# One edge per query in blocks without TensorE, with q, k and v as one paced stream and output projections spread, in a sparse graph attention layer

## The chip, the cores and the metric

The kernel runs on one core of one Trainium2 chip. The metric is the device time of one execution in microseconds (us), lower is better. PE is TensorE, DVE is VectorE, ACT is ScalarE, POOL is GpSimd; SP is the engine whose queue issues the plain DMAs.

## The reference

One graph attention layer on 16 batches of 1024 nodes with 512 features, 8 heads of 64, all float32. Each query attends only to the nodes that the 0/1 matrix `adj` (1024 x 1024, the same for all batches) names in its row:

```python
q = (x @ Wq + bq).reshape(b, n, H, HD)
k = (x @ Wk + bk).reshape(b, n, H, HD)
v = (x @ Wv + bv).reshape(b, n, H, HD)
scores = jnp.einsum('bqhd,bkhd->bhqk', q, k) / jnp.sqrt(jnp.float32(HD))
scores = scores + (1.0 - adj)[None, None, :, :] * -1000000000.0
attn = jax.nn.softmax(scores, axis=-1)
out = jnp.einsum('bhqk,bkhd->bqhd', attn, v).reshape(b, n, d)
return out @ Wo + bo
# and around it
x = _layernorm(x + _L0_gnn_ref(x, adj, ...), axis=-1)
```

The inputs' `adj` has 4043 ones in 1024 x 1024. They are unevenly spread: the first 128 queries have 1404, the last 128 have 273, the largest row has 66, and 60 rows have none (there the softmax is uniform over all nodes, and the attention output is the mean of v).

## The kernel before, in words

It does not form the score matrix. The ones of `adj` are a list of edges (query, key). The 1024 queries are cut into 8 tiles of 128; the edges of tile t, in the order of their queries, are cut into `BLOCKS[t]` blocks of 128 edges, one edge to a partition. The table is (11, 6, 4, 4, 3, 3, 3, 3), 37 blocks a batch and 592 in all. A query without edges has one made-up edge, to a row N of the key table that holds zeros and the mean of v.

`edges(t)` runs once, in the first microseconds and into batch 0: from the rows of `adj` it makes `key_row` and `query_row` (for each edge the row to fetch) and `sums` (for each block a 128 x 128 matrix of zeros and ones that adds up the edges of one query).

For each batch, `front(b, t)` computes q, k and v of one tile of 128 nodes: four matmuls of 128 x 512 each for q, k and v (`product`, L377), a bias, and a write to tables in DRAM (`q_rows`, `kv_rows`, two of each, taken in turn by `b % 2`). DVE adds the biases of q and k (`out_q`, `out_k`), ACT copies v and squares q and k for a guard.

For each block n, these steps follow one another, each in its own turn of a loop:
- `gather(n)`: POOL issues two indirect DMAs, the q row of each edge (`qg`, L501) and its k and v row (`kvg`, L506), eight turns ahead.
- `scores(n)`: DVE multiplies q by k (L515) and adds up by head (L517). `exponentials(n)`: ACT takes exp (L522).
- `weigh(n)`: DVE multiplies v by the exponentials (L533); in batch 0 for every second block, and in batch 15 for two of three, ACT does it (L529).
- `add_up(n)`: PE multiplies the block's matrix from `sums` with the weighted v and the exponentials, in two matmuls (L545, L546), into the PSUM tile `sum` of the query tile.

After the last block of a query tile, `normalise` on DVE divides by the sum of the exponentials (L553, L554, L557). PE transposes the result (`poT`, L566), and `finish(b, t)` multiplies it by Wo (`po`, again L377). DVE adds x (L468) and takes mean and variance; POOL takes the root (L477), ACT scales (L482), SP writes the tile out. The tile of x for this is loaded again by `load_y` (tile `y`), and POOL adds the output bias to it (L461).

The order on every engine is written out by the loop at the end (`tc.manual_schedule()`), with one turn for each block; `later(k, fn)` puts work into a turn further on. In each turn the loop emits the block steps, then takes units of PE work from two lists while a credit lasts: `fronts` (a unit is one matmul of 128 x 512, or a transpose of x) and `finishing`. The credit of a turn (`share`) is set anew for each batch so that the lists run empty with the batch. `finishing` is only filled when `fronts` is empty, so each batch runs the fronts of the next batch first, and then the output projections one after the other. A first stretch of 34 turns without blocks (`LEAD_IN`) makes the edges, the fronts of batch 0 and part of batch 1.

PSUM has eight banks: two `sum` tiles of two banks each and four `fill` tiles of one bank, which all other matmuls share.

## Time and profile before

| | |
|---|---|
| median of 3 runs | 2595.01 us (2594.36 to 2597.61) |
| the profiled execution's own time, and its span | 2595.89 us, 2594.1 us |
| mean granted TensorE clock over the span | 0.982 |
| busy: PE, DVE, POOL, ACT | 2477.6, 1968.2, 1499.0, 698.7 us |
| 16 DMA engines: share of POOL's queue, of SP's queue | 56.3%, 21.2% |
| chain that ended last: PE, POOL, DVE, issue | 68%, 11%, 10%, 7% |

The span runs from the first to the last instruction. In the profile a float32 matmul is two PE instructions, so 512 matmuls of one kind stand as x1024. The spans of two matmuls in a row overlap, since they are pipelined: what a matmul costs PE when it is packed is the distance from its start to the next one's start. The blocks of batch 0 begin at 162.4 us, those of batch 1 at 309.5, and a batch takes about 153.5 us from then on; the last batch begins at 2458.5 us.

### The profile page before, as it was taken

The numbers are of one execution on the slowest core, as the hardware profiler recorded it, in microseconds if no ns is written. First come the engines' busy times: TensorE is split into PE (matmuls) and PEld (weight loads), VectorE is DVE, ScalarE is ACT, GpSimd is POOL, SyncE is SP. The second block draws the span as 40 slices with busy tenths as digits, with TensorE's granted clock in tenths as the row PEclk, the third lists the DMA queues.
The fourth block names the chain that finished last, engine by engine and source line by source line (L and its number), as shares of the span: only waits on it lengthen the run. The fifth ranks groups of instructions, "written<-read, shape, count | busy, mean of one in ns | idle before, by whom it ended". The sixth has DMA issues, their size and how long they took to land.

```text
span 2594.1 us, 26742 instructions
## 1 busy us (share of the span) xinstructions
PE 2477.6 (96%) x7659; PEld 1352.6 (52%) x7659; DVE 1968.2 (76%) x3613; ACT 698.7 (27%) x1764; POOL 1499.0 (58%) x1717
## 2 busy tenths in 40 slices
PE   6988999999999999999999999999999999999967
PEld 3545555555555555555555555555555555555534
DVE  5668778778778877877777777877877777787766
ACT  1345322222222222222222222222222222222254
POOL 0156755647566574756647465564756557475675
PEclk9989999999999999999999999999999999999978
DMA  4368887887879788787878878787887978878785
GB/s 154 110 243 290 270 291 247 286 270 271 283 237 307 254 291 267 257 292 244 301 253 292 271 235 306 244 294 256 277 288 233 309 251 287 264 256 287 230 277 179
DMA packets 228679, 678.01 MB, mean 261 GB/s; under 512 B 29454, under 2 KB 29466, under 8 KB 228524
## 3 DMA queue, kind: packets, MB, share of 16 engines
q0 software_dynamic: 132608, 465.64, 56.3%
q1 hardware_dynamic: 93344, 205.60, 21.2%
q10 hardware_dynamic: 2572, 4.99, 0.5%
q8 instruction: 62, 1.02, 0.2%
q14 instruction: 93, 0.76, 0.1%
HBM read 541.86 MB, written 134.25 MB: 261 GB/s over the span
## 4 chain that ended last, share of the span: by engine, by line
PE 68%; POOL 11%; DVE 10%; issue 7%; ACT 2%; DMA 1%; ACTq 0%; POOLq 0%; another core or an unknown queue 0%; SPq 0%; DVEq 0%
PE pv L377 16%; PE pk L377 15%; PE pq L377 15%; PE sum L546 7%; PE sum L545 7%; POOL kvg L506 4%; PE po L377 4%; POOL y L461 3%; POOL qg L501 2%; DVE y L468 2%; DVE stats L471 2%; PE pxT L359 2%; PE poT L566 2%; DVE qg L515 1%; DVE pv L533 1%
## 5 line engine op out<-in xcount | busy, mean ns | idle before, releaser
L501 POOL DMA_INDIRECT qg<-q_rows,query_row x592 | 586.9, 991 | 588.1 <-DVE s L517 453.7
L506 POOL DMA_INDIRECT kvg<-kv_rows,key_row x592 | 588.7, 994 | 195.2 <-issue 182.9
L533 DVE TENSOR_TENSOR pv<-kvg,pv 128x512 f32<-128x512 f32 x550 | 394.3, 717 | 223.1 <-ACT pv L522 146.8
L377 PE MATMUL pq<-wq,xT 128*128 128x512 f32 x1024 | 482.7, 597 | 14.7 <-ACT xT L363 13.2
L377 PE MATMUL pk<-wk,xT 128*128 128x512 f32 x1024 | 488.9, 598 | 7.1 <-ACT xT L363 7.1
L377 PE MATMUL pv<-wv,xT 128*128 128x512 f32 x1024 | 479.1, 593 | 0.0
L377 PE MATMUL po<-wo,oT 128*128 128x512 f32 x1024 | 473.9, 602 | 0.0
L515 DVE TENSOR_TENSOR qg<-qg,kvg 128x512 f32<-128x512 f32 x592 | 432.6, 731 | 0.3 <-issue 0.3
L517 DVE TENSOR_REDUCE s<-qg 128x8 f32<-128x512 f32 x592 | 406.1, 686 | 20.5
L545 PE MATMUL sum<-pv,sums 128*128 128x256 f32 x1184 | 361.6, 387 | 46.4 <-DVE pv L533 33.8
L545 PEld LDWEIGHTS sum<-pv,sums 128*128 128x128 f32 x1184 | 222.2, 192 | 326.5 <-issue 239.0
L522 ACT ACTIVATE pv<-s 128x8 f32<-128x8 f32 x592 | 124.1, 210 | 929.2 <-DVE s L517 626.5
L546 PE MATMUL sum<-pv,sums 128*128 128x264 f32 x1184 | 366.6, 392 | 4.6 <-ACT pv L529 2.3
L377 PEld LDWEIGHTS pk<-wk,xT 128*128 128x128 f32 x1024 | 194.3, 192 | 193.3 <-issue 175.7
L377 PEld LDWEIGHTS po<-wo,oT 128*128 128x128 f32 x1024 | 192.9, 194 | 182.6 <-issue 173.3
L377 PEld LDWEIGHTS pv<-wv,xT 128*128 128x128 f32 x1024 | 190.5, 191 | 167.0 <-issue 158.4
L377 PEld LDWEIGHTS pq<-wq,xT 128*128 128x128 f32 x1024 | 187.1, 192 | 159.2 <-issue 135.0
L546 PEld LDWEIGHTS sum<-pv,sums 128*128 128x128 f32 x1184 | 226.2, 192 | 41.6 <-ACT pv L529 6.4
L461 POOL TENSOR_TENSOR y<-y,bo_bc 128x512 f32<-128x512 f32 x128 | 163.4, 1277 | 141.5 <-ACT pv L522 74.7
L468 DVE TENSOR_TENSOR y<-po,y 128x512 f32<-128x512 f32 x128 | 88.0, 688 | 151.5 <-POOL y L461 139.4
L404 DVE TENSOR_TENSOR kv<-pk,bk_bc 128x512 f32<-128x512 f32 x128 | 88.2, 689 | 115.8 <-PE pk L377 87.2
L389 DVE TENSOR_REDUCE nrm<-sq 128x8 f32<-128x512 f32 x256 | 172.9, 676 | 1.4 <-ACT sq L388 1.4
(98 smaller groups left out, 1664.8 us busy)
## 6 DMA issues: line engine op xcount, KB each, us to landing
kv_rows<-kv SPq DMA_DIRECT2D x128, 512.0 KB
x<-in_x_dram SPq DMA_DIRECT2D x128, 256.0 KB
q_rows<-q SPq DMA_DIRECT2D x128, 256.0 KB
y<-in_x_dram SPq DMA_DIRECT2D x128, 256.0 KB
out_dram<-y SPq DMA_DIRECT2D x128, 256.0 KB
qg<-q_rows,query_row POOLq DMA_INDIRECT x592
kvg<-kv_rows,key_row POOLq DMA_INDIRECT x592
a<-in_adj_dram SPq DMA_DIRECT2D x8, 512.0 KB
```

What stands on the lines that cost most here:

```text
L377: nc.tensor.matmul(p, lhs()[:, ts(c, P)], w[:, c, :], start=(c == 0), stop=(c == NPAIR - 1))
L389: later(1, lambda: nc.vector.tensor_reduce(NRM[b][:, i, t, :], sq.rearrange("p (h d) -> p h d", d=HD), axis=AX.X, op=OP.add))
L461: later(2, lambda: nc.gpsimd.tensor_tensor(Y[b, t], Y[b, t], bo_bc, op=OP.add))
L468: nc.vector.tensor_tensor(y, p, y, op=OP.add)
L501: nc.gpsimd.indirect_dma_start(out=QG[n], out_offset=None, in_=q_rows[b % 2], in_offset=bass.IndirectOffsetOnAxis(ap=query_row[:, g:g + 1] ...
L506: nc.gpsimd.indirect_dma_start(out=KG[n], out_offset=None, in_=kv_rows[b % 2], in_offset=bass.IndirectOffsetOnAxis(ap=key_row[:, g:g + 1], ...
L515: nc.vector.tensor_tensor(m, m, KG[n][:, 0:D], op=OP.mult)
L517: nc.vector.tensor_reduce(S[n], m.rearrange("p (h d) -> p h d", d=HD), axis=AX.X, op=OP.add)
L522: nc.scalar.activation(PV[n][:, D:], S.pop(n), AF.Exp)
L533: nc.vector.tensor_tensor(pv[:, 0:D].rearrange("p (h d) -> p h d", d=HD), v[:, D:].rearrange("p (h d) -> p h d", d=HD), pv[:, D:, None].to ...
L545: nc.tensor.matmul(SUM[b, t][:, 0, 0:HD2], m, pv[:, 0:HD2], **kw)
L546: nc.tensor.matmul(SUM[b, t][:, 1, 0:HD2 + HEADS], m, pv[:, HD2:], **kw)
```

## The change

**The first edge of each query.** `edges` now gives the first edge of every query (with the made-up edges) a block of its own for each tile, in which edge and query stand on the same partition. Only the others go to the blocks with a `sums` matrix, and the table falls to (10, 5, 3, 3, 2, 2, 2, 2): 29 blocks with PE and 8 without, again 37 a batch. The block without PE is the last of its tile. Its q rows are a plain tile of `q_rows`, so SP loads them with a plain DMA; its k and v rows are gathered by POOL as before. It is scored and weighed as all blocks are (its `PV` has a pool of its own, `pv0`). `normalise`, now in the turn of that block, adds it to the PSUM sums on DVE and then divides.

**Places without an edge.** Where a block is not full, `key_row` is now 65536 instead of 0, and the gather of k and v has a limit of row N, beyond which nothing is fetched. The eight buffers of `kvg` are set to zero by POOL at the start.

**The order.** The fronts of all 16 batches are one list. The share of a turn now also pays for the sums (the constant `SUM` for each block with PE), and it is set so that the fronts run one batch and 14 turns (`EARLY`) ahead of the blocks' batch. Output projections no longer wait for an empty list: a tile's units come first once it is done and its `y` is loaded, at the least two turns after the tile before began; `y` is loaded for one tile at a time. The DRAM tables are three each (`ROWS`). PSUM has one `sum` tile and six `fill` tiles. `y` has 6 buffers (was 7), `oT` 5 (was 7).

```diff
-BLOCKS = (11, 6, 4, 4, 3, 3, 3, 3)
+BLOCKS = (10, 5, 3, 3, 2, 2, 2, 2)
+NO_ROW = 65536.0
+ROWS = 3
+EARLY = 14
+SUM = 0.87
...
-    NB = sum(BLOCKS)
+    NS = sum(BLOCKS)
+    NB = NS + NT
...
-            return psum.tile([P, HALF], F32, tag="fill", name=name, bufs=4)
+            return psum.tile([P, HALF], F32, tag="fill", name=name, bufs=6)
...
+            nc.vector.tensor_scalar(off, kl[:, 0:1], -1.0, 0.0, op0=OP.add, op1=OP.max)
+            nc.vector.tensor_scalar(key_row[:, NS + t:NS + t + 1], off, float(N), None, op0=OP.min)
...
+                nc.vector.tensor_scalar(e[:, 0, :], e[:, 1, :], 0.0, NO_ROW, op0=OP.is_lt, op1=OP.mult)
+                nc.vector.tensor_tensor(key_row[:, g0:g0 + n], e[:, 1, :], e[:, 0, :], op=OP.max)
...
+            if i == BLOCKS[t]:
+                g = NS + t
+                nc.sync.dma_start(QG[n], q_rows[b % ROWS][ds(t * P, P), :])
+            else:
+                g = first[t] + i
+                nc.gpsimd.indirect_dma_start(
+                    out=QG[n], out_offset=None, in_=q_rows[b % ROWS],
+                    in_offset=bass.IndirectOffsetOnAxis(ap=query_row[:, g:g + 1], axis=0),
+                )
...
                 in_offset=bass.IndirectOffsetOnAxis(ap=key_row[:, g:g + 1], axis=0),
+                bounds_check=N, oob_is_err=False,
...
-                SUM[b, t] = psum.tile([P, 2, HALF], F32, tag="sum", name=f"sum_{b}_{t}", bufs=2)
+                PSUM[b, t] = psum.tile([P, 2, HALF], F32, tag="sum", name=f"sum_{b}_{t}", bufs=1)
...
-            nc.vector.tensor_scalar(r, s[:, 1, HD2:HD2 + HEADS], 1.0e-30, None, op0=OP.max)
+            nc.vector.tensor_tensor(r, s[:, 1, HD2:HD2 + HEADS], pv[:, D:], op=OP.add)
+            nc.vector.tensor_tensor(
+                o.rearrange("p (a d) -> p a d", a=2), s[:, :, 0:HD2], pv[:, 0:D].rearrange("p (a d) -> p a d", a=2),
+                op=OP.add,
+            )
             nc.vector.reciprocal(r, r)
-            for i in range(2):
-                nc.vector.tensor_tensor(
-                    o[:, ts(i, HD2)].rearrange("p (h d) -> p h d", d=HD),
...
+            o8 = o.rearrange("p (h d) -> p h d", d=HD)
+            nc.vector.tensor_tensor(o8, o8, r[:, :, None].to_broadcast([P, HEADS, HD]), op=OP.mult)
...
+        for i in range(8):
+            nc.gpsimd.memset(work.tile([P, 2 * D], F32, tag="kvg", name=f"kvg_first_{i}", bufs=8), 0.0)
...
+                    left = sum(u[0] for u in fronts)
+                    goal = fronts_time - (n // NB + 2 + EARLY / NB) * batch_time
+                    share = (max(0.0, left - goal) + NT * NPAIR * PRODUCT + NS * SUM) / NB
...
+                if 0 <= n < total and blocks[n][2] == BLOCKS[blocks[n][1]]:
+                    normalise(n)
...
-                    if not fronts and not finishing and done and n > loaded.get(done[0], n):
+                    if not finishing and done and n > loaded.get(done[0], n) and n > last_finish + 1:
```

How it moves the engines' orders is seen at three places in the middle of batch 8. In the rows, the numbers in a name are batch and tile (`sum_8_6`: batch 8, tile 6) or the block (`pv_327`), and the last number tells buffers apart.

PE, tile 6 of batch 8, before. This stands late in the batch, where the fronts are used up:

```order
L545 MATMUL sum_8_6_10063<-pv_327_9978,sums_108 128x256
L546 MATMUL sum_8_6_10063<-pv_327_9978,sums_108 128x264
L377 MATMUL po_8_1_10025<-wo_69,oT_8_1_9708 128x512 x2
L377 MATMUL po_8_2_10070<-wo_69,oT_8_2_9813 128x512
L545 MATMUL sum_8_6_10063<-pv_328_10017,sums_108 128x256
L546 MATMUL sum_8_6_10063<-pv_328_10017,sums_108 128x264
L566 MATMUL poT_8_5_10099<-ident_58,o_8_5_10051 128x128 x4
L377 MATMUL po_8_2_10070<-wo_69,oT_8_2_9813 128x512 x3
L377 MATMUL po_8_3_10107<-wo_69,oT_8_3_9918 128x512
L545 MATMUL sum_8_6_10063<-pv_329_10061,sums_108 128x256
L546 MATMUL sum_8_6_10063<-pv_329_10061,sums_108 128x264
```

and the same tile now:

```order
L571 MATMUL sum_8_6_10750<-pv_327_10687,sums_108 128x256
L572 MATMUL sum_8_6_10750<-pv_327_10687,sums_108 128x264
L391 MATMUL po_8_4_10753<-wo_69,oT_8_4_10685 128x512
L591 MATMUL poT_8_5_10755<-ident_58,o_8_5_10705 128x128 x4
L391 MATMUL po_8_4_10753<-wo_69,oT_8_4_10685 128x512 x2
L571 MATMUL sum_8_6_10750<-pv_328_10721,sums_108 128x256
L572 MATMUL sum_8_6_10750<-pv_328_10721,sums_108 128x264
L391 MATMUL po_8_4_10753<-wo_69,oT_8_4_10685 128x512
L391 MATMUL pv_10_1_10728<-wv_67,xT_10_1_10497 128x512 x2
L373 MATMUL pxT_10_3_10785<-ident_58,x_10_3_10379 128x128 x4
L391 MATMUL pq_10_2_10826<-wq_63,xT_10_2_10656 128x512 x4
```

The third pair of sums of the tile is gone; units of a later batch's fronts (`pq_10_2`) and one tile's projection (`po_8_4`) stand between the sums, where three tiles' projections stood.

DVE, at the end of tile 5 of batch 8, before:

```order
L533 TENSOR_TENSOR pv_328_10017<-kvg_328_9830,pv_328_10017 128x512
L515 TENSOR_TENSOR qg_329_9854<-qg_329_9854,kvg_329_9856 128x512
L517 TENSOR_REDUCE s_329_10042<-qg_329_9854 128x8
L553 TENSOR_SCALAR rden_8_5_10048<-sum_8_5_9957 128x8
L554 RECIPROCAL rden_8_5_10048<-rden_8_5_10048 128x8
L557 TENSOR_TENSOR o_8_5_10051<-sum_8_5_9957,rden_8_5_10048 128x256 x2
L468 TENSOR_TENSOR y_8_0_9960<-po_8_0_9992,y_8_0_9960 128x512
```

and now:

```order
L559 TENSOR_TENSOR pv_327_10687<-kvg_327_10485,pv_327_10687 128x512
L537 TENSOR_TENSOR qg_328_10510<-qg_328_10510,kvg_328_10512 128x512
L539 TENSOR_REDUCE s_328_10703<-qg_328_10510 128x8
L579 TENSOR_TENSOR rden_8_5_10706<-sum_8_5_10662,pv_326_10660 128x8
L580 TENSOR_TENSOR o_8_5_10705<-sum_8_5_10662,pv_326_10660 128x512
L584 RECIPROCAL rden_8_5_10706<-rden_8_5_10706 128x8
L586 TENSOR_TENSOR o_8_5_10705<-o_8_5_10705,rden_8_5_10706 128x512
L484 TENSOR_TENSOR y_8_3_10629<-po_8_3_10665,y_8_3_10629 128x512
```

Two instructions of 128 x 512 stand where two of 128 x 256 stood, one turn earlier than before, and the final addition of tile 3 (`y_8_3`) follows directly, where it was tile 0's.

POOL now, from the second block of tile 5 of batch 8 on (`kvg_326` is the block without PE; before, a gather of `qg` stands ahead of every gather of `kvg`):

```order
L522 DMA qg_325_10417<-q_rows_2_118,query_row_110 128x512
L527 DMA kvg_325_10419<-kv_rows_2_115,key_row_109 128x1024
L477 TENSOR_TENSOR y_8_1_10385<-y_8_1_10385,bo_bc_72 128x512
L527 DMA kvg_326_10454<-kv_rows_2_115,key_row_109 128x1024
L493 TENSOR_TENSOR rstd_10435<-rstd_10435,neg_half_88 128x1
L494 TENSOR_TENSOR rstd_10435<-rstd_10435,mv_10432 128x1
L495 TENSOR_TENSOR rstd_10435<-rstd_10435,neg_one_90 128x1
L522 DMA qg_327_10483<-q_rows_2_118,query_row_110 128x512
```

The gather of `qg_326` is no longer on POOL; SP issues that load instead.

More of the change, by code (lines that the diff above doesn't have):

```diff
@@ L519, in exponentials @@
         def exponentials(n):
[L521 removed]
+            b, t, i = blocks[n]
+            if i == BLOCKS[t]:
+                PV[n] = work.tile([P, D + HEADS], F32, tag="pv0", name=f"pv_{n}", bufs=2)
+            else:
+                PV[n] = work.tile([P, D + HEADS], F32, tag="pv", name=f"pv_{n}", bufs=4)
             nc.scalar.activation(PV[n][:, D:], S.pop(n), AF.Exp)
@@ L585 @@
         with tc.manual_schedule():
-            gathered = 0
-            fronts, finishing = [], []
-            front_batches = 0
+            fronts = transpose_x(0, 0) + transpose_x(0, 1)
+            for b in range(B):
+                for t in range(NT):
+                    fronts += front(b, t)
+            fronts_time = sum(u[0] for u in fronts)
+            batch_time = fronts_time / B
+            finishing, last_finish = [], -LEAD_IN
             credit = 0.0
@@ L595 @@
                 now[0] = n
-                if front_batches < B and front_batches <= max(n // NB, 0) + 1:
-                    fronts += [u for t in range(NT) for u in front(front_batches, t)]
-                    front_batches += 1
                 if n < 0:
@@ L602 @@
                 elif n % NB == 0:
-                    tiles = len(done) + (NT if n + NB < total else NT + 2)
-                    share = (sum(u[0] for u in fronts) + tiles * NPAIR * PRODUCT) / NB
-                while gathered < min(n + AHEAD + 1, total) and blocks[gathered][0] in set_up:
-                    gather(gathered)
-                    gathered += 1
+                    left = sum(u[0] for u in fronts)
+                    goal = fronts_time - (n // NB + 2 + EARLY / NB) * batch_time
+                    share = (max(0.0, left - goal) + NT * NPAIR * PRODUCT + NS * SUM) / NB
+                while gathered[0] < min(n + AHEAD + 1, total) and blocks[gathered[0]][0] in set_up:
+                    gather(gathered[0])
+                    gathered[0] += 1
                 if 0 <= n + 1 < total:
```

82 lines of the change are left out of this document (37 added, 45 removed).

## The prediction

> **What bounds the kernel now.** I read the page's engine lines first, then PE's timeline, then one window for each stage.
>
> ```profile
> PE 2477.6 (96%) x7659; PEld 1352.6 (52%) x7659; DVE 1968.2 (76%) x3613; ACT 698.7 (27%) x1764; POOL 1499.0 (58%) x1717
> PE 68%; POOL 11%; DVE 10%; issue 7%; ACT 2%; DMA 1%; ACTq 0%; POOLq 0%; another core or an unknown queue 0%; SPq 0%; DVEq 0%
> L545 PE MATMUL sum<-pv,sums 128*128 128x256 f32 x1184 | 361.6, 387 | 46.4 <-DVE pv L533 33.8
> L546 PE MATMUL sum<-pv,sums 128*128 128x264 f32 x1184 | 366.6, 392 | 4.6 <-ACT pv L529 2.3
> ```
>
> PE is busy and carries the chain that ended last. But its spans overlap, so their lengths are not prices. The timeline of PE in the middle of a batch (start, length, operation) gives the prices:
>
> ```profile
> 1001.64 0.59 PE L545 MATMUL sum<-pv,sums 128*128 128x256 f32 x2
> 1002.07 0.61 PE L546 MATMUL sum<-pv,sums 128*128 128x264 f32 x2
> 1002.52 3.60 PE L377 MATMUL pv<-wv,xT 128*128 128x512 f32 x8
> 1005.95 0.59 PE L545 MATMUL sum<-pv,sums 128*128 128x256 f32 x2
> 1006.38 0.61 PE L546 MATMUL sum<-pv,sums 128*128 128x264 f32 x2
> 1006.83 0.60 PE L359 MATMUL pxT<-ident,x 128*128 128x128 f32 x4
> 1007.27 2.74 PE L377 MATMUL pq<-wq,xT 128*128 128x512 f32 x6
> ```
>
> From start to start: a block's sums take 1002.52 - 1001.64 = 0.88 us, four matmuls of 512 columns 1005.95 - 1002.52 = 3.43 (0.858 each), four transposes 0.44. Nothing lies between. A batch has 96 matmuls for q, k, v, 32 of `po`, 16 groups of transposes, one mean and 37 sums: 82.4 + 27.5 + 7.0 + 0.9 + 32.6 = 150.3 us of packed PE work. The windows by stage (length, then busy time of PE, PE's loads, DVE, ACT, POOL; clock; DMA share) tell where that is the limit:
>
> ```profile
> 0.00:162.40 162.40, 136.76 (x401) 67.10 (x402) 92.67 (x172) 47.69 (x84) 32.57 (x36) 0.98 0.44 155
> 162.40:309.50 147.10, 127.28 (x423) 73.60 (x422) 118.42 (x247) 73.40 (x232) 96.67 (x97) 0.92 0.79 269
> 309.50:460.00 150.50, 150.50 (x471) 82.90 (x470) 117.47 (x215) 34.80 (x83) 85.81 (x97) 1.00 0.81 268
> 920.30:1073.80 153.50, 151.31 (x470) 82.82 (x470) 121.15 (x217) 36.47 (x86) 92.31 (x106) 1.00 0.82 272
> 2458.50:2476.80 18.30, 10.32 (x25) 5.35 (x25) 9.79 (x19) 10.46 (x38) 14.40 (x21) 0.72 0.80 254
> 2476.80:2573.90 97.10, 72.06 (x211) 39.62 (x210) 67.72 (x126) 54.21 (x209) 66.74 (x77) 0.82 0.74 248
> 2573.90:2594.10 20.20, 11.23 (x33) 5.30 (x31) 8.00 (x27) 3.72 (x5) 7.41 (x15) 0.84 0.31 103
> ```
>
> Batch 1 takes 150.5 us and batch 5 (920.3 to 1073.8) 153.5, against 150.3 of packed work: from batch 1 to 14 the kernel is PE's stream and little else. In batch 0 the order before holds only 118.6 us of PE work at these prices, in 147.1; in batch 15 and the end about 61, in 135.6. There others set the pace.
>
> **The change part by part.**
>
> *Sums removed.* 8 blocks a batch lose their two matmuls: 8 x 0.88 = 7.0 us, and 128 x 0.88 = 112.6 in all. A full batch falls to 143.1 us. By the group rows above the same would be 4 x (0.387 + 0.392) = 3.1 us summed for a block, or 728.2 / 592 = 1.23 as busy time, 157 in all. The Trainium skill ("Perfetto Trace Analysis", its note ahead of "Sequencer Loop") calls matmul busy time a bad metric, because matmuls are pipelined; by busy time the kernel would end 45 us earlier than I say, and the timeline's 0.88 agrees with the page. I take 0.88.
>
> *Addition on DVE.* The timeline of DVE gives its prices:
>
> ```profile
> 1009.40 0.68 DVE L421 TENSOR_TENSOR vsum<-vsum,kv 128x512 f32<-128x512 f32 x1
> 1010.00 0.16 DVE L553 TENSOR_SCALAR rden<-sum 128x8 f32<-128x8 f32 x1
> 1010.20 0.20 DVE L554 RECIPROCAL rden<-rden 128x8 f32<-128x8 f32 x1
> 1010.43 0.75 DVE L557 TENSOR_TENSOR o<-sum,rden 128x256 f32<-128x256 f32 x2
> 1011.11 0.68 DVE L533 TENSOR_TENSOR pv<-kvg,pv 128x512 f32<-128x512 f32 x1
> 1011.71 0.68 DVE L515 TENSOR_TENSOR qg<-qg,kvg 128x512 f32<-128x512 f32 x1
> 1012.42 0.69 DVE L517 TENSOR_REDUCE s<-qg 128x8 f32<-128x512 f32 x1
> 1013.02 0.68 DVE L397 SCALAR_TENSOR_TENSOR q<-pq,bq_bc 128x512 f32<-128x512 f32 x1
> ```
>
> `normalise` takes 1011.11 - 1010.00 = 1.11 us. Now it has two small instructions (0.20 + 0.23) and two of 128 x 512, each between 0.60 (L533) and 0.71 (L515, whose successor needs its result): 1.63 to 1.85, and I take 1.75, nearer to the dependent one. So DVE gets 0.64 x 8 = 5.1 us a batch: 121.2 + 5.1 = 126 in a batch of about 145.6. That is hidden behind PE, with the cover thinner: 87% instead of 79%. Without cover it would cost 16 x 5.1 = 82 us. It is thinnest in the four tiles of three blocks: three blocks at 1.91 us, `normalise`, the layer norm of one tile (1.74 us) and about half a front tile (five instructions at 0.60 a tile, so 1.6) make 10.8 us of DVE beside 11.5 of PE.
>
> *Order.* The boundary of each batch has one stall (timeline, idle time and its releaser in brackets):
>
> ```profile
> 929.33 0.70 PE L545 MATMUL sum<-pv,sums 128*128 128x256 f32 x2 [1.90 <-DVE pv L533]
> 926.85 0.69 DVE L468 TENSOR_TENSOR y<-po,y 128x512 f32<-128x512 f32 x1 [5.37 <-POOL y L461]
> 928.60 0.68 DVE L533 TENSOR_TENSOR pv<-kvg,pv 128x512 f32<-128x512 f32 x1
> 911.08 1.28 POOL L461 TENSOR_TENSOR y<-y,bo_bc 128x512 f32<-128x512 f32 x1
> 916.43 1.27 POOL L461 TENSOR_TENSOR y<-y,bo_bc 128x512 f32<-128x512 f32 x1
> 925.55 1.27 POOL L461 TENSOR_TENSOR y<-y,bo_bc 128x512 f32<-128x512 f32 x1
> DVE y L468 <- POOL y L461: 139.4, 64, 5.4
> POOL y L461 <- DMA y<-in_x_dram: 40.4, 12, 8.2
> ```
>
> In the run of projections one after the other, POOL falls behind (5.3 us from one `y` to the next); DVE then waits 5.37 us for it, and 1.90 reach PE, so DVE runs some 3.5 us ahead. Spread projections give POOL three turns or more for each, and this stall should go. In its place small ones may come, since DVE is fuller and each `y` is loaded only two turns before POOL needs it. I take 2.5 us a batch, between the 0.2 of batch 1 and the 3.2 of batch 5.
>
> *POOL, SP, DMA.* POOL's timeline prices a gather:
>
> ```profile
> 999.98 0.94 POOL L501 DMA_INDIRECT qg<-q_rows,query_row  x1 [1.95 <-DVE s L517]
> 1001.22 0.94 POOL L506 DMA_INDIRECT kvg<-kv_rows,key_row  x1 [0.30 <-issue]
> 152.67 1.95 POOL L506 DMA_INDIRECT kvg<-kv_rows,key_row  x1 [0.30 <-issue]
> 11.39 2.34 POOL L276 TENSOR_TENSOR codes<-a,place 128x1024 f32<-128x1024 f32 x1 [8.07 <-DMA a<-in_adj_dram]
> ```
>
> A gather takes 1.24 us of POOL, start to start; eight fewer a batch free 10 us, so POOL, at 92 of 153.5, gets looser. SP issues the 128 q loads, each in the place where POOL's gather stood, eight turns ahead. Behind them on SP stand writes of q, k, v that themselves wait for DVE's later work of the same turn, so I cost the wait for a free `qg` buffer at nothing; at worst it makes the writes late, which have a whole batch to land. The limit on the gathers is not in the trace. Its bounds are minus the time of the roughly 633 rows a batch that are no longer fetched (3712 places with PE, 3079 edges), and, from above, the longest gather of batch 0 (1.95 us, 1.0 more than the usual one). I take zero: most gathers stand at 0.94, and PE hides either end. The eight memsets of `kvg` stand on POOL ahead of `codes`, in its wait of 8.07 us for `adj`; each writes as many elements as `codes`, which takes 2.34 us, so they cost between nothing and 8 x 2.34 - 8.07 = 10.7 us. I take nothing, since a memset reads nothing, and keep the rest for the range.
>
> *One `sum` tile.* The next tile's first sum waits until `normalise` has read PSUM: one turn (3.9 us) and the lead of 3.5 us against 2.7 of DVE. Nothing, as long as DVE leads.
>
> *Three tables, fronts further ahead.* This moves PE work from the end to batch 0. Counted in the changed order at the prices above, PE has 149.0 us in batch 0 (was 118.6), 136.7 in batch 1, 143.1 on average in 2 to 13, 110.5 in batch 14 and 58 in batch 15. Batch 0's idle PE was 28.5 us, partly three waits for rows of `adj`, such as
>
> ```profile
> 178.30 0.90 PE L338 MATMUL pof<-ident,of 128*128 128x128 f32 x3 [5.89 <-ACT kv L410]
> 222.80 2.08 PE L377 MATMUL pk<-wk,xT 128*128 128x512 f32 x2 [7.15 <-ACT xT L363]
> ```
>
> Those stay, a microsecond shorter each as the turns are longer; the one at the batch's end (about 5.7) goes: 28.5 - 3 - 5.7 = 19.8. The last 51 turns have no fronts, 37 before. There DVE (3.1 us a turn with ACT not helping in batch 14) and POOL set the pace: 3.3 us in the last 14 turns of batch 14, and 97.1 / 33 = 2.94 in batch 15.
>
> The sum of the stages: until batch 0 161 (was 162.4); batch 0 149.0 + 19.8 = 169; batch 1 136.7 + 2.5 = 139; batches 2 to 13 1717 + 12 x 2.5 = 1747; batch 14 86.4 + 1.5 + 14 x 3.3 = 134; batch 15 37 x 2.94 = 109, and the end 20. Together 2479 of span, against 2594.1. The profiled execution took 2595.89 us, 1.8 over its span, and the median of the runs 2595.01, 0.9 over it: 2480 us, 4.4% faster.
>
> **The rivals.**
>
> 1. *DVE becomes the bound in the short tiles.* If each `y` costs DVE its mean wait of 139.4 / 64 = 2.2 us, a three-block tile takes 13.0 us against 11.5, four of them lose 6 us a batch, 3.5 more than I allow, or with the `sum` tile chained behind it up to 6: 13 x 3.5 to 6 gives 2526 to 2558. For it speaks the 94% there; against it that batches 1 to 14 hide all such waits but one.
> 2. *The stalls go altogether.* Batches at 0.2 instead of 2.5, and half of batch 0's waits covered by six `fill` tiles: 2480 - 30 - 10 = 2440.
> 3. *Slower: the `y` chain.* Each tile now goes from load to POOL to DVE at the shortest distance. If each waits as the one at 926.85 does, a batch is 126 + 8 x 5.37 = 169 us of DVE, and the kernel about 2790. It decides against the change from a mean wait of (153.5 - 126) / 8 = 3.4 us; the mean was 2.2.
> 4. *The gather with a limit is dear on POOL.* POOL's work is 66 x 1.24 + 8 x (5.3 - 2.5) = 104 us a batch with its issue gaps; 1.1 us more on each of 37 gathers makes 146, where it starts to bind, and 1.35 eats the whole gain: 2480 to 2600.
> 5. *The end runs at half clock.* The clock is 0.72 to 0.84 in batch 15 and 1.00 in batch 5, and the stretch without fronts grows by 14 turns. At half clock throughout, PE's 24 + 58 us there double to 164, beside 46 + 129 = 175 us that the others need. If they overlap as now, that adds nothing; if half of the added 82 is exposed, the time is 2521. Against it: batch 15 kept its 2.94 us a turn at these clocks. The Trainium skill ("TensorE: Matmul & The Clock Gate", "HAM oscillation") says that gaps of more than about 3.4 us on PE halve its clock; by that rule the added turns run cold too, and the windows agree as far as they go.
>
> **How the numbers follow.** My sum 0.60, rival 1 0.13, rival 2 0.13, rival 3 0.05, rival 4 0.06, rival 5 0.03. For 8 in 10 the range takes in rivals 2 and 5 and most of rival 1: 2440 to 2545. About 0.2% can be told from no change here; slower comes from rival 3 and a third of 4 (0.07), the same from half of 4 (0.03), faster 0.90.
>
> **What would show it.** Right: sums x928 instead of x1184, batches of 144 to 147 us, PE packed in them, the idle stretch in the last 51 turns at 3.0 to 3.3 us each, DVE near 87%. Wrong: PE waiting for `pv` or `o` of DVE in the short tiles (rival 1), DVE waiting for `y` of POOL eight times a batch (3), a longer `kvg` gather (4). The prediction falls if a batch in the middle takes over 150 us.

## The result, and the profile after

| | before | after |
|---|---|---|
| median of 4 runs each | 2596.31 us (2594.36 to 2601.66) | 2467.62 us (2464.03 to 2469.3) |
| span of the profiled execution | 2594.1 us | 2466.9 us |

The ratio is 0.9499 (95% interval 0.9481 to 0.9518): 5.0% faster, where 2480 us and 4.4% were said. The page of the changed kernel (busy time, then the chain by engine, then two groups):

```profile
PE 2354.3 (95%) x7123; PEld 1259.7 (51%) x7123; DVE 2025.7 (82%) x3646; ACT 690.8 (28%) x1764; POOL 1508.0 (61%) x1597
PE 85%; DVE 4%; issue 4%; DMA 3%; POOL 3%; ACT 1%; another core or an unknown queue 0%; SPq 0%; POOLq 0%; DVEq 0%; ACTq 0%
L571 PE MATMUL sum<-pv,sums 128*128 128x256 f32 x928 | 287.4, 392 | 66.6 <-DVE rden L584 44.5
L527 POOL DMA_INDIRECT kvg<-kv_rows,key_row x592 | 652.1, 1101 | 201.1 <-issue 171.7
```

PE's share of the chain went from 68% to 85%, and POOL's and DVE's from 21% to 7%. The windows tell where (same columns as before: length; busy time of PE, its loads, DVE, ACT, POOL; clock; DMA share). The first is batch 5; the next four are batch 14 until its fronts end, its last 14 turns, and the last batch in two pieces:

```profile
896.70:1040.10 143.40, 143.40 (x439) 76.92 (x438) 120.11 (x211) 35.79 (x85) 93.93 (x98) 1.00 0.82 273
2187.40:2275.00 87.60, 87.60 (x270) 48.16 (x269) 72.88 (x125) 22.02 (x54) 56.06 (x61) 1.00 0.80 265
2275.00:2325.00 50.00, 30.66 (x82) 17.05 (x80) 39.71 (x80) 7.77 (x23) 34.75 (x40) 0.82 0.76 248
2325.00:2440.00 115.00, 77.94 (x209) 44.08 (x210) 77.54 (x140) 63.24 (x243) 72.81 (x79) 0.81 0.64 215
2440.00:2466.90 26.90, 10.43 (x27) 4.84 (x25) 7.14 (x23) 3.03 (x4) 5.65 (x11) 0.76 0.13 42
```

To count what PE must do in a stage, I multiply the number of its matmuls there with the prices from the timeline (0.88 us a pair of sums, 0.858 a matmul of 512 columns, 0.44 four transposes). What the stage takes beyond this is called idle below; it includes matmuls that ran at less than full clock.

| stage (us) | before: length, idle | after: length, idle | said for after |
|---|---|---|---|
| until batch 0 | 162.4, 33.5 | 160.0, 32.4 | 161 |
| batch 0 | 147.1, 28.0 | 167.5, 18.5 | 169, 19.8 |
| batch 1 | 150.5, 0.3 | 137.0, 0.3 | 139, 2.5 |
| batches 2 to 13, sum | 1846.1, 44.4 | 1723.0, 5.6 | 1747, 30 |
| batch 14 | 152.4, 3.1 | 137.6, 27.1 | 134 |
| batch 15 and the end | 135.6, 64.7 | 141.9, 78.0 | 129 |

The middle is now nothing but PE: 143.4 us for 143.1 of packed work. The waits from 464 to 2187 us (us in all, times, longest), PE's list whole and the first three rows of DVE's:

```profile
PE sum L571 <- DVE rden L584: 1.5, 2, 1.0
...
DVE y L484 <- POOL y L477: 79.5, 39, 4.6
DVE pv L559 <- ACT pv L548: 67.0, 84, 2.8
DVE kv L420 <- PE pk L391: 24.8, 18, 2.1
```

DVE still waits some 80 us for `y` of POOL in these twelve batches, in 39 pieces, and no more than 1.5 us of all its waits reach PE. Before, from 309 to 2458 us, PE's wait for DVE and DVE's for `y`:

```profile
PE sum L545 <- DVE pv L533: 26.8, 15, 1.9
...
DVE y L468 <- POOL y L461: 120.7, 59, 5.4
```

This is the thing to read here: the same kind of wait, no shorter on average (2.0 us in both), now costs nothing. What is gone is the one wait of 5.4 us that stood at the end of each batch; of those that are left only two are over 4 us, and they hardly ever use up DVE's lead over PE.

### The profile page after: what moved, and what is told of

Read it like the earlier page. It is cut to its first block, busy times and chain, and to the rows that moved or that the text cites. A ratio compares the mean times of both kernels' runs of the same rounds, so it can differ in the third digit from the quotient of the medians.

```text
span 2466.9 us, 26129 instructions
## 1 busy us (share of the span) xinstructions
PE 2354.3 (95%) x7123; PEld 1259.7 (51%) x7123; DVE 2025.7 (82%) x3646; ACT 690.8 (28%) x1764; POOL 1508.0 (61%) x1597
## 2 busy tenths in 40 slices
DMA packets 236873, 636.53 MB, mean 258 GB/s; under 512 B 39583, under 2 KB 39595, under 8 KB 236718
## 4 chain that ended last, share of the span: by engine, by line
PE 85%; DVE 4%; issue 4%; DMA 3%; POOL 3%; ACT 1%; another core or an unknown queue 0%; SPq 0%; POOLq 0%; DVEq 0%; ACTq 0%
PE po L391 16%; PE pq L391 16%; PE pv L391 16%; PE pk L391 16%; PE sum L572 8%; PE sum L571 7%; PE poT L591 2%; PE pxT L373 2%; POOL kvg L527 1%; DMA y<-in_x_dram 1%; POOL qg L522 1%; DMA kvg<-kv_rows,key_row 1%; POOL codes L284 1%; DVE qg L537 1%; ACT pv L555 1%
## 5 line engine op out<-in xcount | busy, mean ns | idle before, releaser
L527 POOL DMA_INDIRECT kvg<-kv_rows,key_row x592 | 652.1, 1101 | 201.1 <-issue 171.7
L522 POOL DMA_INDIRECT qg<-q_rows,query_row x464 | 486.0, 1047 | 383.4 <-DVE s L539 233.1
L391 PE MATMUL po<-wo,oT 128*128 128x512 f32 x1024 | 487.6, 601 | 0.5 <-ACT y L498 0.5
L391 PE MATMUL pk<-wk,xT 128*128 128x512 f32 x1024 | 482.2, 595 | 0.0
L537 DVE TENSOR_TENSOR qg<-qg,kvg 128x512 f32<-128x512 f32 x592 | 416.2, 703 | 0.0
L571 PE MATMUL sum<-pv,sums 128*128 128x256 f32 x928 | 287.4, 392 | 66.6 <-DVE rden L584 44.5
L571 PEld LDWEIGHTS sum<-pv,sums 128*128 128x128 f32 x928 | 176.1, 194 | 279.6 <-issue 196.8
L572 PE MATMUL sum<-pv,sums 128*128 128x264 f32 x928 | 291.2, 396 | 1.2 <-ACT pv L555 0.7
L391 PEld LDWEIGHTS pq<-wq,xT 128*128 128x128 f32 x1024 | 185.9, 191 | 167.5 <-issue 148.8
L572 PEld LDWEIGHTS sum<-pv,sums 128*128 128x128 f32 x928 | 179.9, 195 | 30.7 <-ACT pv L555 4.0
L493 POOL TENSOR_TENSOR rstd<-rstd,neg_half 128x1 f32<-128x1 f32 x128 | 103.9, 812 | 80.4 <-DVE rstd L490 66.7
```

The source lines that it names most:

```text
L391: nc.tensor.matmul(p, lhs()[:, ts(c, P)], w[:, c, :], start=(c == 0), stop=(c == NPAIR - 1))
L493: nc.gpsimd.tensor_tensor(rstd[:, 0:1], rstd[:, 0:1], neg_half, op=OP.pow)
L522: nc.gpsimd.indirect_dma_start(out=QG[n], out_offset=None, in_=q_rows[b % ROWS], in_offset=bass.IndirectOffsetOnAxis(ap=query_row[:, g:g + ...
L527: nc.gpsimd.indirect_dma_start(out=KG[n], out_offset=None, in_=kv_rows[b % ROWS], in_offset=bass.IndirectOffsetOnAxis(ap=key_row[:, g:g + ...
L537: nc.vector.tensor_tensor(m, m, KG[n][:, 0:D], op=OP.mult)
L571: nc.tensor.matmul(PSUM[b, t][:, 0, 0:HD2], m, pv[:, 0:HD2], **kw)
```

## The experiments

### The parts of the change apart

**The blocks alone**: the changed kernel, with the old order, and the old numbers of tables and buffers, put back.

```diff
-ROWS = 3
+ROWS = 2
...
-            for b in range(B):
-                for t in range(NT):
-                    fronts += front(b, t)
...
+                if front_batches < B and front_batches <= max(n // NB, 0) + 1:
+                    fronts += [u for t in range(NT) for u in front(front_batches, t)]
-                    if not finishing and done and n > loaded.get(done[0], n) and n > last_finish + 1:
+                    if not fronts and not finishing and done and n > loaded.get(done[0], n):
```

> The blocks without PE alone: new blocks, limit and normalise as in the changed kernel, but the order of before (fronts of one batch, then its projections in a run; two DRAM tables; two sum tiles and four fill tiles; y 7, oT 7). Theory 1 (PE's stream is the time, each pair of sums is worth 0.88 us): batches 1 to 14 fall from 153.5 to about 146.5 us, batch 0 and 15 stay: 2594 - 14 x 7.0 = about 2497 us. Rival (the order brought the gain, DVE's added work eats most of the sums): batches at 150 or more, 2550 us or above.

Measured: 2633.76 us, ratio 1.015 (1.0134 to 1.0165), slower than before by 1.5%. I had said 2497 or thereabouts. A batch in the middle (the window of batch 6), PE's waits from 460 to 2400 us (first row), and one of the stalls in the timelines of PE, DVE and POOL:

```profile
1091.70:1248.60 156.90, 146.64 (x438) 78.29 (x439) 124.54 (x217) 36.42 (x86) 90.70 (x98) 0.97 0.78 249
```

```profile
PE sum L570 <- DVE pv L558: 136.5, 13, 12.7
```

```profile
920.74 0.61 PE L571 MATMUL sum<-pv,sums 128*128 128x264 f32 x2
934.00 1.19 PE L570 MATMUL sum<-pv,sums 128*128 128x256 f32 x2 [12.65 <-DVE pv L558]
931.43 0.69 DVE L483 TENSOR_TENSOR y<-po,y 128x512 f32<-128x512 f32 x1 [6.25 <-POOL y L476]
914.35 1.28 POOL L476 TENSOR_TENSOR y<-y,bo_bc 128x512 f32<-128x512 f32 x1
920.12 1.28 POOL L476 TENSOR_TENSOR y<-y,bo_bc 128x512 f32<-128x512 f32 x1
930.13 1.27 POOL L476 TENSOR_TENSOR y<-y,bo_bc 128x512 f32<-128x512 f32 x1
```

PE's packed work falls to 143.1 us as said, but each batch ends in one stall of up to 12.7 us, and what follows the stall runs slower (clock 0.97). The run of projections at the batch's end is paced by POOL, 5.8 us from one `y` to the next and 10 at the last. Before, the same run had a wait of 1.90 us for PE, and DVE one of 5.37; I read it so: with the sums taken out, PE is through its own part sooner and DVE's wait of 6.25 comes late to it, so that the 7.0 us saved stand at the batch's end as waiting. PE's timelines show one thing more. Before, seven matmuls for q and k stand right ahead of the sums that wait (from 921.26 to 927.44 us); here nothing does, and PE stands still from the sums at 920.74 on. Of this batch's 156.9 us PE waits 10.3 (156.90 - 146.64), and 3.5 more are matmuls at the lower clock (146.64 - 143.1); in batch 5 before it was 2.2 and 1.0 (153.50, 151.31 and 150.3). The 10.6 us more are, within the rounding, the 7.0 us saved and the 3.4 us by which a batch is longer.

**The order alone**: all blocks with PE as before, two `sum` tiles and gathers without a limit, with the changed kernel's one list of fronts, head start, spacing and three tables.

Against the kernel before:

```diff
+ROWS = 3
+EARLY = 14
...
+            for b in range(B):
+                for t in range(NT):
+                    fronts += front(b, t)
...
+                    goal = fronts_time - (n // NB + 2 + EARLY / NB) * batch_time
...
-                    if not fronts and not finishing and done and n > loaded.get(done[0], n):
+                    if not finishing and done and n > loaded.get(done[0], n) and n > last_finish + 1:
...
```

> The order alone: one list of fronts, projections spread, three tables, EARLY 14, y 6, oT 5, with the 37 blocks of before (all with PE) and two sum tiles and four fill tiles. Theory 1: PE stays packed, so batches 2 to 13 fall from 153.8 to 150.5 us (the stall at the boundary goes, -40 us), and batch 0 gets denser while the end gets longer: about 2560 us. Rival (spreading is worth nothing or the end eats it): 2590 us or more. Rival (order brought the gain): 2500 us or less.

Measured: 2557.41 us, ratio 0.9851 (0.9835 to 0.9866), as said. A batch of the middle:

```profile
932.50:1083.00 150.50, 150.50 (x472) 83.06 (x471) 124.81 (x225) 36.09 (x86) 94.82 (x106) 1.00 0.83 278
```

It is PE without a gap: 150.5 us for 150.1 of packed work. Now the two parts can be set side by side, as differences of medians: the blocks alone +38 us, the order alone -39, both -129. The blocks are worth 90 us once the order is changed and less than nothing without it.

**PE's work given back**: the changed kernel with a pair of products of the sums' size in every block without PE, into an unused tile.

```diff
+            BACK[n] = pv
...
+                elif 0 <= n < total:
+                    pv, p = BACK.pop(n), fill_psum(f"back_{n}")
+                    nc.tensor.matmul(p[:, 0:HD2], ident, pv[:, 0:HD2], start=True, stop=True)
+                    nc.tensor.matmul(p[:, 0:HD2 + HEADS], ident, pv[:, HD2:], start=True, stop=True)
```

> The changed kernel with the removed work given back to TensorE alone: for each block without TensorE, two products of the sums' size into an unused tile, from which nothing is read. Theory: TensorE bounds batches 1 to 13 and the pair costs what it costs elsewhere, 0.88 us, so a batch grows by 8 x 0.88 = 7.0 us to 150.3 us, and the total by 13 x 7.0 = 91 us, in the first batch and the last two by nothing to 7 us: 2556-2570 us. Rival: what the change saved was the waits at the tile's end rather than TensorE's time; then the pair fits where TensorE now waits and the total stays below 2510 us.

Measured: 2559.5 us, ratio 0.9872 (0.9857 to 0.9888), +92 us over the changed kernel.

```profile
922.30:1072.70 150.40, 150.40 (x471) 83.21 (x470) 124.39 (x218) 36.05 (x87) 89.81 (x97) 1.00 0.80 257
```

A batch is 7.0 us longer, which is 8 x 0.88. So the start-to-start price is what a pair costs; by its summed durations (1.23 us) it would have been 9.8.

**The gathers' limit taken away**: places without an edge fetch row 0 of the tables, as before.

```diff
-                nc.vector.tensor_scalar(e[:, 0, :], e[:, 1, :], 0.0, NO_ROW, op0=OP.is_lt, op1=OP.mult)
-                nc.vector.tensor_tensor(key_row[:, g0:g0 + n], e[:, 1, :], e[:, 0, :], op=OP.max)
+                nc.vector.tensor_scalar(key_row[:, g0:g0 + n], e[:, 1, :], float(N), None, op0=OP.min)
...
-                bounds_check=N, oob_is_err=False,
```

> The changed kernel without the limit on the gathers: empty places fetch row 0, as before (633 rows of 4 KB more in each batch). Theory (DMA and POOL are hidden behind PE): no change, 2467 us within 5, batches at 143.4; the mean kvg gather shows whether the limit made it longer (1101 ns with it, 994 before). Rival (the skipped rows are part of the gain): 2480 us or more.

Measured: 2467.68 us, ratio 0.9507 (0.9494 to 0.952), no difference. The traffic of the changed kernel (its gathers stand above, at 1101 ns), then gathers and traffic without the limit:

```profile
DMA packets 236873, 636.53 MB, mean 258 GB/s; under 512 B 39583, under 2 KB 39595, under 8 KB 236718
```

```profile
L526 POOL DMA_INDIRECT kvg<-kv_rows,key_row x592 | 610.0, 1030 | 198.9 <-issue 158.0
DMA packets 236869, 677.94 MB, mean 275 GB/s; under 512 B 29455, under 2 KB 29467, under 8 KB 236718
```

The limit saves 41.4 MB (the 633 rows a batch are 16 x 633 x 4096 bytes = 41.5). POOL's gathers are 0.07 us longer with it. Neither is on the path.

### Where the blocks' gain went in the old order

**The blocks alone, without POOL's addition to `y`** (the output bias is then left out).

```diff
-            later(2, lambda: nc.gpsimd.tensor_tensor(Y[b, t], Y[b, t], bo_bc, op=OP.add))
```

> The new blocks in the old order (2633.8 us), with GpSimd's addition of the output bias to each y tile left out (1.3 us each, 128 of them; the bias is then missing from the output). Theory: in the old order the eight output projections of a batch stand in one run at its end, one about every 4.3 us of TensorE's time, while GpSimd needs 5.3 to 5.8 us for what each of them asks of it (two gathers, the addition, three small operations on the deviation); its gathers then come late and TensorE waits 13 us once in each batch. Without the addition GpSimd needs some 4 us for each and keeps up: batches 1 to 14 fall from 157 to 144-149 us, the total to 2440-2520 us. Rival: the stall comes from VectorE, which waits for the projections in order and then has the tile's scores and weights to make up; it stays, batches stay above 153 us and the total above 2590 us.

Measured: 2517.7 us, ratio 0.9704 (0.9689 to 0.9719): 116 us less than with the addition. Batch 9, and PE's waits from 460 to 2400 us:

```profile
1492.80:1642.80 150.00, 146.49 (x439) 78.56 (x439) 119.87 (x217) 36.33 (x86) 77.89 (x91) 0.98 0.80 261
```

```profile
PE sum L569 <- DVE pv L557: 47.0, 13, 4.3
```

The stall falls from 10.5 to 3.6 us a batch. So POOL's backlog in the run of projections makes most of it, though not all: batches settle at 150 us, above the 144 to 149 that I had said, and 3.6 us of waiting with some matmuls at a lower clock behind it stay. What makes this rest I did not separate.

**The head start of the stream**: 6 turns instead of 14, in the kernel with the later y, whose own run follows below (2453.63 us).

```diff
-EARLY = 14
+EARLY = 6
```

> The kernel with the later y at the end (2453.6 us), with the stream of q, k and v 6 turns ahead of its batch and not 14. Theory: a batch's last rows are written some 31 turns into the batch before, and its means about three turns later, while its first gathers are wanted 8 turns ahead, at turn 29, and its first scores at turn 35: the gathers start late, VectorE waits for them once in every batch, and TensorE with it, for 3 to 12 us: batches 1 to 13 of 147-155 us, and the end shorter by up to 10 us: 2490-2590 us. Rival: the gathers have enough time in hand even then, batches stay at 143.5 us, and only the end gets shorter, since more of the stream lies where TensorE waits: 2435-2452 us.

Measured: 2605.97 us, ratio 1.0045 (1.003 to 1.006). All that the change brought is lost, more than I had said: batches 2 to 13 take 145.7 to 167.3 us, with 3 to 23 us idle. DVE's first and third row of waits from 460 to 2300 us, and POOL's second:

```profile
DVE y L484 <- POOL y L477: 173.9, 45, 11.1
...
DVE qg L537 <- DMA kvg<-kv_rows,key_row: 60.3, 16, 5.8
...
POOL y L477 <- DMA y<-in_x_dram: 152.5, 51, 6.5
```

The late gathers that the theory named are there (60.3 us), but other waits grew more. In the kernel with the later y, in the same window, DVE waits 91.8 us for POOL's `y` (now 173.9), POOL 100.2 for loads of `y` (now 152.5), and POOL 38.0 for DVE's `rstd` (now 188.4, POOL's first row). So DVE and POOL wait for each other more than before. Which of these waits starts the others was not tried.

### What hides behind PE in the middle

**Three more products of 128 x 512 per tile on DVE**, into an unused tile (24 a batch at 0.68 us, 16.4 us).

```diff
+                if 0 <= n < total and blocks[n][2] < 3:
+                    junk = work.tile([P, D], F32, tag="junk", name=f"junk_{n}", bufs=1)
+                    nc.vector.tensor_tensor(junk, bq_bc, bk_bc, op=OP.mult)
```

> The changed kernel with one product of 128x512 more on VectorE in the first three turns of every tile, into an unused tile: 3 x 0.70 us, 24 in a batch, 16.8 us. Theory: VectorE (120 of 143.4 us busy in a middle batch) has the room for it on average, 137 of 143.4 us, and the two turns that it works ahead smooth the short tiles; batches 2 to 13 stay within 1 us of 143.4 us, and only the first batch and the last two, where TensorE already waits, grow, by 5 to 20 us in all: 2470-2490 us. Rival: VectorE is the bound inside the short tiles already and the average hides it; then nearly all of the dose shows, 12 x 8 us and more: above 2560 us.

Measured: 2519.81 us, ratio 0.9709 (0.9695 to 0.9723), 52 us more than the changed kernel, between the two expectations. Batch 6, and PE's waits from 460 to 2200 us:

```profile
1060.00:1207.10 147.10, 144.49 (x439) 76.51 (x439) 140.97 (x241) 36.71 (x87) 96.20 (x99) 1.00 0.82 267
```

```profile
PE sum L571 <- DVE rden L584: 21.0, 15, 3.3
PE sum L571 <- DVE pv L559: 7.8, 16, 1.1
```

Batches 2 to 13 grew from 1723.0 to 1768.6 us, 3.8 us each: of 16.4 us added, 12.6 disappear behind PE. In batch 6 DVE is 96% busy then, and PE, 98% busy, has begun to wait for it.

**The same with two `sum` tiles.**

The second tile takes two banks of PSUM, so the `fill` tiles fall from six to four.

```diff
-            return psum.tile([P, HALF], F32, tag="fill", name=name, bufs=6)
+            return psum.tile([P, HALF], F32, tag="fill", name=name, bufs=4)
...
-                PSUM[b, t] = psum.tile([P, 2, HALF], F32, tag="sum", name=f"sum_{b}_{t}", bufs=1)
+                PSUM[b, t] = psum.tile([P, 2, HALF], F32, tag="sum", name=f"sum_{b}_{t}", bufs=2)
```

> The kernel with three more products per tile on VectorE (2519.8 us, batches of 144.0 to 150.9 us, VectorE 95 to 96% busy), with two sum tiles and four tiles for the other products. Theory: what showed of the dose came through the one sum tile: TensorE's first sums of a tile stand for VectorE's normalising of the last (21.0 us in 15 recorded waits from 460 to 2200 us); with a second tile they need not, batches 2 to 13 fall to 143.4-145 us and the total to 2475-2495 us. Rival: a VectorE so full is late with the weights themselves, and TensorE then waits for those instead: batches keep an average above 146 us, total 2505-2525 us.

Measured: 2523.35 us, ratio 0.9716 (0.9703 to 0.973), no gain. PE's waits from 460 to 2200 us, the first two rows:

```profile
PE poT L591 <- DVE y L484: 17.0, 13, 2.2
PE sum L571 <- DVE pv L559: 10.7, 15, 1.6
```

The wait for the normalised tile is gone, and another one for DVE stands in its place. It comes from the edit's other half. One of the 13 waits, in the timelines of DVE and PE:

```profile
1944.34 0.69 DVE L586 TENSOR_TENSOR o<-o,rden 128x512 f32<-128x512 f32 x1
1946.14 0.68 DVE L484 TENSOR_TENSOR y<-po,y 128x512 f32<-128x512 f32 x1
1946.88 0.66 PE L591 MATMUL poT<-ident,o 128*128 128x128 f32 x4 [2.21 <-DVE y L484]
```

The transposes `poT` read `o`, which is ready about 1.8 us before they start; they begin when `y` has read its projection. What ties them to `y` is the `fill` tile that this frees: they write into one. It is so in all 13, and with six `fill` tiles there is no such row. So this run does not show what a second `sum` tile would be worth by itself.

### The last 51 turns

**Two `sum` tiles, four `fill` tiles** in the changed kernel (the edit above).

> The changed kernel with two sum tiles and four fill tiles, as before. Theory: in the last 51 turns PE's first sum of a tile waits for normalise (42.9 us in 10 waits), because there is one sum tile; with two this goes, the turns there fall from 3.2 to about 2.9 us, and batches 1 to 13 stay at 143.4: 2450 to 2460 us, unless batch 0 loses up to 10 us for the two fill tiles. Rival (POOL, DMA or the cold clock set the pace of the end): no change, 2467 us within 5.

Measured: 2470.57 us, ratio 0.9516 (0.9502 to 0.9529): no gain; the theory that the one tile sets the pace of the end fell. The waits from 2275 us on, the first two rows of PE and the first of DVE in the changed kernel, then with two tiles:

```profile
PE sum L571 <- DVE rden L584: 42.9, 10, 7.7
PE sum L571 <- DVE pv L559: 5.1, 3, 4.0
...
DVE y L484 <- PE po L391: 24.9, 8, 5.9
```

```profile
PE poT L591 <- DVE o L586: 19.4, 8, 4.2
PE sum L571 <- DVE pv L559: 16.5, 7, 5.5
...
DVE y L484 <- PE po L391: 23.2, 7, 6.0
```

PE's wait moved from the sums to the transposes and the weights. Here the new waits are for results (`o`, `pv`) and not for a `fill` tile: the row that names a wait tells which instruction met the late engine first, not what would be won by removing that dependency. What stayed is DVE's own wait, for the projection.

**The later y**: at the end, DVE takes a projection's result two turns after its issue.

```diff
-                    later(1, lambda: out(p))
+                    later(2 if late and not fronts else 1, lambda: out(p))
...
-            return product(f"po_{b}_{t}", lambda: OT[b, t], W["o"], out)
+            return product(f"po_{b}_{t}", lambda: OT[b, t], W["o"], out, late=True)
```

> The changed kernel, where, once the stream of q, k and v is at its end, VectorE takes an output projection's result two turns after it is issued and not one. Theory: in the last 50 turns TensorE and VectorE wait for each other in turn: VectorE stands up to 3 us at each y for the projection's last product, which runs 4.2 to 5.2 us there instead of 3.43 us, and TensorE then stands for VectorE's weights and the normalised tile. A turn more takes the first of the two waits away: eleven tiles by 1 to 2 us, total 2445-2460 us. Rival: as with two sum tiles, the wait only moves to the next operation of the chain: 2464-2470 us.

Measured: 2453.63 us (2452.48 to 2455.88), ratio 0.9458 (0.9445 to 0.9471), 14 us below the changed kernel, as said. The waits again, PE's first row and the fourth of DVE:

```profile
PE sum L571 <- DVE rden L584: 29.9, 8, 7.6
...
DVE y L484 <- PE po L391: 2.5, 1, 2.5
```

DVE's wait for the projection falls from 24.9 to 2.5 us, and PE's for DVE with it. Batch 14 takes 133.7 us instead of 137.6, batch 15 with the end 131.0 instead of 141.9: in-order engines were waiting for each other in turn, and one turn of distance loosens the ring. PE's wait for ACT's weights grows meanwhile, from 2.5 to 10.3 us. The last run below is as fast; no kernel here is faster.

**The later y and two `sum` tiles.**

> The kernel with the later y at the end (2453.6 us), and two sum tiles again with four tiles for the other products. Theory: with VectorE no longer standing at each y, the wait of TensorE for the normalised tile (29.9 us in 8 waits of the last 190 us) is the one left in the chain, and a second sum tile, which was worth nothing while the other wait held, takes most of it away: 2430-2446 us; the middle batches stay at 143.4 us. Rival: two sum tiles are worth nothing here either, since the sums then wait for the weights of the next block: 2450-2458 us.

Measured: 2457.2 us, ratio 0.9468 (0.9455 to 0.9481). Again nothing: batch 15 with the end takes 133.2 us, where it took 131.0. PE's sums now wait for the weights (19.8 us for ACT's and 15.6 for DVE's from 2275 us on), as the rival said.

**The later y, and one more product on TensorE in each of the last 51 turns.**

```diff
+                if not fronts and n < total:
+                    p = fill_psum(f"warm_{n}")
+                    for c in range(1):
+                        nc.tensor.matmul(p, ident, W["o"][:, c, :], start=True, stop=True)
```

> The kernel with the later y at the end (2453.6 us), and in each of the last 51 turns, where no q, k or v is left, one product of 128x512 more on TensorE into an unused tile (0.86 us at full clock, 44 us in all; their result is not read). Theory: TensorE's granted clock in the last batch (0.80) comes from its idle stretches, and the products that run at less than full clock are part of the chain there; kept busier, the clock rises above 0.9, a projection's four products fall from 4.2-5.2 us to about 3.5 us, and the end gets shorter by 5 to 20 us: 2433-2449 us. Rival: the clock is no link of the chain, or the added products stand in its way: 2453-2480 us.

Measured: 2453.36 us, ratio 0.9453 (0.9438 to 0.9468), the same. Batch 15 with the end, first with the later y alone, then with the products added:

```profile
2323.10:2454.10 131.00, 84.63 (x234) 46.16 (x234) 90.55 (x167) 66.41 (x247) 79.83 (x94) 0.80 0.62 203
```

```profile
2320.70:2451.70 131.00, 104.51 (x308) 55.91 (x308) 90.49 (x166) 66.34 (x247) 79.17 (x93) 0.91 0.62 203
```

The clock rises from 0.80 to 0.91, PE does 32 us more of packed work, and the stretch is 131.0 us in both. A warmer clock, bought this way, wins nothing. From 2275 us on DVE waits for PE only 7.0 us with the later y (2.5 for projections, 4.5 for sums) and 7.1 with the products, so that a faster PE has little to give there. How much the products took back of what the clock gave, this run does not separate.

## Why the prediction was right

- **What bounds the kernel, and the price of the sums.** Right. Giving the pairs back costs 7.0 us a batch, the 0.88 us of the timeline.
- **Addition on DVE.** 0.64 us more per tile was said, and 0.40 is what it is. The changed `normalise` in DVE's timeline:

```profile
2276.58 0.16 DVE L579 TENSOR_TENSOR rden<-sum,pv 128x8 f32<-128x8 f32 x1
2276.65 0.68 DVE L580 TENSOR_TENSOR o<-sum,pv 128x512 f32<-128x512 f32 x1
2277.25 0.20 DVE L584 RECIPROCAL rden<-rden 128x8 f32<-128x8 f32 x1
2277.48 0.69 DVE L586 TENSOR_TENSOR o<-o,rden 128x512 f32<-128x512 f32 x1
2278.09 0.68 DVE L403 TENSOR_REDUCE nrm<-sq 128x8 f32<-128x512 f32 x1
```

  From 2276.58 to 2278.09 are 1.51 us, below even the lower bound of 1.63: the first small instruction is followed after 0.07 us, since the next does not need its result, and I had priced it at 0.20. DVE's share of the twelve middle batches is 1473.77 / 1723.0 = 86% (84% in batch 5), where 87% was said.
- **Order.** This is one of the two terms that were mis-sized. The stall at the boundary goes, as said; I allowed 2.5 us a batch for small ones in its place, and they are 0.3 in most batches, 5.6 us in the twelve instead of 30. That is 24 us too many, of a total error of 12. The 2.5 came from DVE being fuller; the added products show how much room was left: of 16.4 us a batch more, 12.6 were hidden. Rival 2 (2440 us) had this term right. It missed by the end (16 us), which it shares with my sum, and by batch 0, where it had half of PE's waits covered (8 us).
- **The parts as a sum.** The prediction priced the sums and the order as two terms to be added. They are not: without the order the sums bring a loss of 38 us. The forecast could add them only because both were there. Rival 3, the one that ends slower, put a loss on the `y` chain in the new order; there its waits stay hidden, but in the old order the same chain makes most of the loss (116 us come back without POOL's addition).
- **The end.** 3.3 us a turn was said for the last 14 turns of batch 14; they took 50.0 / 14 = 3.6. Batch 15 with its end took 141.9 us and not 129. I had carried over 2.94 us a turn from before. The step that failed is the view of a pace that DVE and POOL set: DVE is busy for only 77.54 of 115 us there. What sets it, in part, is that PE and DVE wait for each other at the turn in which DVE meets the projection, since the later y gives 14 us back; what sets the rest stays open. The 16 us of this term and the 24 of the one above had opposite signs: that the total is nearer than its parts is luck. A slip beside it: PE's packed work in batch 15 and the end was counted at about 61 us before and 58 after, and is 71 and 64 by the table (135.6 - 64.7, 141.9 - 78.0). It enters only the price of rival 5.
- **Batch 0, tables, POOL, SP, DMA, the one `sum` tile, the limit.** 167.5 us against 169, and zero for the rest, as said: the limit was tried, and a second `sum` tile at the price of two `fill` tiles, and neither can be told from no change. The loads that SP took over, the tables and POOL's memsets were not tried apart.
- **Rivals 1 and 4.** PE waits 1.5 us for DVE in twelve batches, so DVE did not become the bound. The gathers of k and v are longer by 0.07 us for the limit, where rival 4 needed 1.1.
- **Rival 5.** The clock is 0.76 to 0.82 in the last 51 turns, but a warmer one brought nothing in the trial with the later y. The Trainium skill ("TensorE: Matmul & The Clock Gate", "HAM oscillation") has long gaps on PE lower its clock, and the trace agrees (behind a gap of 7.69 us the sums take twice their usual time, shown below). That the time follows is not seen here, where PE mostly waits for others.

## What to carry to other kernels

Before taking work off the engine that bounds a kernel, look in each stage for where the next engine has room when that work is gone: the same edit lost 38 us in an order with one crowded run per batch, and won 90 in an order where the same work was spread. An engine's waits are no loss as long as it runs far enough ahead of the one that bounds: here DVE at 86% hid nearly all of them, and at 95% no longer. Where two in-order engines wait for each other in turn, try one stage more between issue and use: it was worth 14 us here. A second `sum` tile, paid for with two `fill` tiles, was worth nothing; at the end it moved the wait to the next row, and in the middle the missing `fill` tiles made a new one.

## What the runs showed of the hardware

Gaps of 2.4 us and less, one after the other, were enough to lower PE's clock. At the end of the kernel with the later y (timeline of PE):

```profile
2346.31 1.22 PE L571 MATMUL sum<-pv,sums 128*128 128x256 f32 x2 [2.38 <-ACT pv L555]
2347.32 1.19 PE L572 MATMUL sum<-pv,sums 128*128 128x264 f32 x2
```

These two usually take 0.59 and 0.61 us. Behind a gap of 2.38 us, with several of 0.3 to 1.6 us in the ten ahead of it, they take twice that; the granted clock is 0.86 from 2342 to 2346 us, where PE is busy for 1.41 of 4 us, and 0.50 from 2346 to 2350. The Trainium skill ("TensorE: Matmul & The Clock Gate", "HAM oscillation") tells of gaps over about 3.4 us; no single gap here is that long. In the changed kernel the sums behind a gap of 7.69 us do the same, which agrees with the page of the Trainium skill:

```profile
2289.60 1.19 PE L571 MATMUL sum<-pv,sums 128*128 128x256 f32 x2 [7.69 <-DVE rden L584]
```

An indirect gather with rows beyond its limit does not move them, and is still no shorter on POOL: 1101 ns on average, against 1030 when the same places fetch row 0. Nor are there fewer packets: 236873 against 236869. With the limit 10128 more of them are under 512 B, which is the number of the skipped rows (16 x 633), so that each skipped row seems still to send a small packet.
